# First attention pair of a fused kernel: products opened by the first matmul, zero-point term added by VectorE behind them

## The chip, the cores and the metric

The kernel runs on one core of a Trainium2 chip. Its engines are named as the profile names them: PE (TensorE, with PEld for its weight loads), DVE (VectorE), ACT (ScalarE), POOL (GpSimd) and SP (SyncE, which issues most DMAs). The metric is the device time of one execution in microseconds, as the median of several runs; less is better. Single instructions and stretches come from one execution that the hardware profiler recorded.

## What is computed

For each of two batches, an integer-quantised product of the layer-normalised x with a context matrix is added to x, and then a dense layer with LoRA terms is applied to the layer norm of that:

```python
def fake_quant(x, scale, zp):
    q = jnp.clip(jnp.round(x / s + z), 0.0, 255.0)
    return (q - z) * s
...
q1 = fake_quant(_layernorm(x), x1_scale, x1_zp)
q2 = fake_quant(ctx_4096, x2_scale, x2_zp)
x = x + jnp.matmul(q1, q2)
x = x + ffn(_layernorm(x), gate, kernel, bias, lora_A, lora_B, lora_A_shared, lora_B_shared)
```

x is (2, 1024, 2048), the context (2, 2048, 2048), all in float32. The change touches only the first part, and of it only the first of 32 products of its kind.

## The kernel before

**Tiles.** The 1024 tokens of a batch are eight tiles of 128, in four groups g of two tiles. The 2048 columns of the context are four blocks n of 512. A pair (b, n, g) is one call of `xattn_pair`: for each of the two token tiles j of group g, 16 matmuls over k = 0..15 (the 2048 inner rows in steps of 128) into one PSUM bank of 512 columns; the two banks are one tile `pa`.

**Operands.** The integers are centred at 128 so that both operands are exact in bf16. `prep_x` makes the left operand for one token tile: statistics on DVE (L283, L257), the short chain L259 to L290 on DVE with a square root on ACT (L261), quantisation on ACT (L295, to uint8 in the working tile `wk`; then L298 twice, to bf16 with row sums), 16 transposes on PE (L303) and two copies on DVE (L304) into `c1T[g]`; L307 and L308 make `r_s`, the tile's row sums times the context's offset. `quantise` makes the right operand, a slice r of two k steps at a time: ACT L314 from the loaded float slice in `lit` to int16 in `q2b`, DVE L317 from there to bf16 in `c2`. Eight slices make a block.

**Buffers.** `q2b` has three buffers, which `take` and `give` hand out in turn in the program's order. `quantise` takes one for each slice; `column_term` takes one between the slices of block 0 and those of block 1.

**Column term.** `column_term` (L327 to L348) sums the columns of a block: 16 narrow matmuls (`pcp`, L333), a copy on DVE into a q2b buffer (L343), one fp32 product with `mean_w` (`pc`, L345), and DVE L348, which scales it and adds a constant: `colt[n]`.

**The opening.** With zero points z1 and z2 a product is the centred product plus a term of the row and a term of the column. Before each group of 16 matmuls ACT writes this sum, `colt[n] + r_s[m]`, into the bank (L359), and the matmuls add to it, all with `start=False`. Behind the pair, DVE scales the two banks and adds them to x (L370), and takes statistics for the second norm (L372).

**Order.** For batch 0 the program calls, in this order: `prep_x` of tile 0, the eight slices of block 0 with `prep_x` of tile 1 after the fourth, the loads of x tiles 4 to 7, `column_term` of block 0, pair (0,0,0), slices 0 to 3 of block 1, `prep_x` of tiles 2 and 3, pair (0,0,1), the other slices and the column term of block 1, pairs (0,1,0) and (0,1,1); then tiles 4 to 7 with their pairs. `tc.issue_after(opened.ins)` sets the DVE instructions of tiles 4 to 7 behind the first pair's L370. The order on each engine's queue is not simply that of the program: a planner that works when the kernel is built sets it from the program's order, from what each instruction waits for and from its own costs, so that an instruction that it takes to be ready goes ahead of an earlier one that is not. In the trace, for instance, transposes of tile 3 stand among the first products of pair (0,0,1).

Of the kernel before, what the change touches and what calls it, by code (L numbers as in the profile page):

```python
# [14 lines left out]
AF = mybir.ActivationFunctionType  # L15
ALU = mybir.AluOpType
# [50 lines left out]
def tile_quant_xattn_then_lora_ffn(  # L67
# [17 lines left out]
    nc = tc.nc  # L85
# [11 lines left out]
    MG = GT // P  # L97
# [28 lines left out]
    r_s = const.tile([P, MT], F32, tag="r_s", name="r_s")  # L126
# [9 lines left out]
    def bf(t, n):  # L136

        return t.rearrange("p k n -> p (k n)").bitcast(BF16).rearrange("p (k n) -> p k n", n=n)
# [46 lines left out]
    def load_x(b, m, cols=slice(0, D)):  # L185
        nc.sync.dma_start(out=y[m // MG][:, m % MG, cols], in_=x[b, ds(m * P, P), cols])
# [90 lines left out]
    def prep_x(b, m, c1T, wk):  # L277

        nm = f"{b}_{m}"
        g, tok = m // MG, ds((m % MG) * P, P)  # L280
        ym = y[g][:, m % MG, :]
        for n in range(NN):
            nc.vector.bn_stats(st1[:, m, n, :], ym[:, ds(n * NB, NB)])  # L283
        mean, rstd = norm_stats(st1[:, m], f"a{nm}")

        k = small.tile([P, 1], F32, tag="kx", name=f"kx_{nm}")
        nc.vector.tensor_mul(k, rstd, inv1)
        o = small.tile([P, 1], F32, tag="ox", name=f"ox_{nm}")
        nc.vector.tensor_mul(o, mean, k)
        nc.vector.tensor_sub(o, z1, o)  # L290

        wf = flat(wk)
        q8 = wf[:, ds((m % 2) * (D // 4), D // 4)].bitcast(U8)
        qh = wf[:, D // 2 : D].bitcast(BF16)
        nc.scalar.activation(q8, ym, AF.Identity, bias=o, scale=k)  # L295
        rsum = small.tile([P, 2], F32, tag="rsum", name=f"rsum_{nm}")
        for h in range(2):
            nc.scalar.activation(  # L298
                qh[:, ds(h * H, H)], q8[:, ds(h * H, H)], AF.Identity, bias=n_centre, accum_out=rsum[:, h : h + 1]
            )  # L300
            pt = ps_m.tile([P, KH, P], BF16, tag="pm", name=f"pt_{nm}_{h}")
            for kt in range(KH):
                nc.tensor.transpose(pt[:, kt, :], qh[:, ds(h * H + kt * P, P)], ident_h)  # L303
            nc.vector.tensor_copy(c1T[g][:, ds(h * KH, KH), tok], pt)  # L304

        r_c = small.tile([P, 1], F32, tag="r_c", name=f"r_c_{nm}")
        nc.vector.tensor_add(r_c, rsum[:, 0:1], rsum[:, 1:2])  # L307
        nc.vector.tensor_mul(r_s[:, m : m + 1], r_c, d2)  # L308

    def quantise(c2, r):  # L310

        buf, t = next_loaded()
        qi = q2b.take()
        nc.scalar.activation(qi, t, AF.Relu, bias=z2, scale=inv2)  # L314
        lit.give(buf)
        load_next()
        nc.vector.tensor_scalar(c2[r // 4][:, ds(2 * (r % 4), 2), :], qi, QMAX, CENTRE, ALU.min, ALU.subtract)  # L317
        q2b.give(qi)
# [5 lines left out]
    colt = {}  # L324
    pairs = []

    def column_term(b, n, c2):  # L327


        parts = ps_m.tile([P, NB], F32, tag="pm", name=f"pcp_{b}_{n}")  # L330
        for k in range(KT):
            row = P // 4 * (k % 4)
            nc.tensor.matmul(  # L333
                parts[row : row + P // 4, :],
                ones_h[:, 0 : P // 4],
                c2[k // 8][:, k % 8, :],
                start=(k < 4),
                stop=(k >= KT - 4),
                skip_group_check=True,
            )  # L340
        st = q2b.take()
        sf = st.rearrange("p k n -> p (k n)").bitcast(F32)
        nc.vector.tensor_copy(sf, parts)  # L343
        pc = ps_m.tile([P, NB], F32, tag="pm", name=f"pc_{b}_{n}")
        nc.tensor.matmul(pc, mean_w, sf, start=True, stop=True)  # L345
        q2b.give(st)
        colt[n] = bp.take()
        nc.vector.tensor_scalar(colt[n], pc, d1, kdd, ALU.mult, ALU.add)  # L348

    def xattn_pair(b, n, g, c1T, c2):  # L350

        cols = ds(n * NB, NB)
        pairs.append((b, n, g))
        pa = ps_acc.tile([P, MG, NB], F32, tag=("acc0", "acc1", "delta")[len(pairs) % 3], name=f"pa_{b}_{n}_{g}")
        for j in range(MG):

            m = g * MG + j
            with tc.high_priority():
                nc.scalar.activation(pa[:, j, :], colt[n], AF.Identity, bias=r_s[:, m : m + 1])  # L359
            for k in range(KT):  # L360
                nc.tensor.matmul(  # L361
                    pa[:, j, :],
                    c1T[g][:, k, ds(j * P, P)],
                    c2[k // 8][:, k % 8, :],
                    start=False,
                    stop=(k == KT - 1),
                    skip_group_check=True,
                )
        yp = y[g][:, :, cols]
        summed = nc.vector.scalar_tensor_tensor(yp, pa, s12, yp, ALU.mult, ALU.add)  # L370
        for j in range(MG):
            nc.vector.bn_stats(st2[:, g * MG + j, n, :], y[g][:, j, cols])  # L372
        return summed
# [315 lines left out]
    c1T = [bf(t, GT) for t in c1T_bufs]  # L689
    wk = big.take()  # L690
    c2b = {}
    c2 = {}

    def open_c2(n):
        c2b[n], c2[n] = take_c2()
# [5 lines left out]
    for b in range(B):  # L701
# [6 lines left out]
        if b == 0:  # L708
            open_c2(0)
            prep_x(0, 0, c1T, wk)  # L710
            for r in range(NR):
                quantise(c2[0], r)
                if r == 3:
                    prep_x(0, 1, c1T, wk)
            for m in range(4, MT):
                load_x(0, m)
            open_c2(1)
            column_term(b, 0, c2[0])
        opened = xattn_pair(b, 0, 0, c1T, c2[0])
        if b == 0:  # L720
            for r in range(4):
                quantise(c2[1], r)
            for m in (2, 3):
                prep_x(b, m, c1T, wk)
        xattn_pair(b, 0, 1, c1T, c2[0])
        if b == 0:
            for r in range(4, NR):
                quantise(c2[1], r)
            column_term(b, 1, c2[1])
        for g in range(2):  # L730
            xattn_pair(b, 1, g, c1T, c2[1])
# [131 lines left out]
        if b + 1 < B:  # L863
            c1T_bufs, c1T, wk = state["c1b"], state["c1T"], state["wk"]
# [53 lines left out]
```

## Time and profile before

| | us |
|---|---|
| median of 3 runs (lowest to highest) | 1123.19 (1122.52 to 1124.55) |
| the profiled execution's own time | 1122.67 |
| its span, first instruction to last | 1120.9 |
| PE busy in the span | 1066.2 |
| DVE busy | 745.5 |
| ACT busy | 261.6 |
| pair (0,0,0): products on PE, first to last | 41.36 to 51.05 |
| mean of one L361 matmul, 128x512 bf16 (x992) | 0.381 |
| mean of one L359 opening, 128x512 (x64) | 0.683 |
| mean of one L370, 128x1024 (x32) | 1.282 |

The page gives for each engine its busy time and a row of 40 digits, each for 28 us of the span; other views list instructions in order of time, with the idle time before each and what ended it in square brackets, or sum up chosen stretches. A matmul's duration there contains its passage through the pipelined array, so that sixteen matmuls of 0.38 us take 3.61 us together. Some matmul records are missing, so a count can be short by a few per cent.

### The profile page before, as it was taken

The numbers are of one execution on the slowest core, as the hardware profiler recorded it, in microseconds if no ns is written. First come the engines' busy times: TensorE is split into PE (matmuls) and PEld (weight loads), VectorE is DVE, ScalarE is ACT, GpSimd is POOL, SyncE is SP. The second block draws the span as 40 slices with busy tenths as digits, with TensorE's granted clock in tenths as the row PEclk, the third lists the DMA queues.
The fourth block names the chain that finished last, engine by engine and source line by source line (L and its number), as shares of the span: only waits on it lengthen the run. The fifth ranks groups of instructions, "written<-read, shape, count | busy, mean of one in ns | idle before, by whom it ended". The sixth has DMA issues, their size and how long they took to land.

```text
span 1120.9 us, 10622 instructions
## 1 busy us (share of the span) xinstructions
PE 1066.2 (95%) x3898; PEld 493.9 (44%) x3930; DVE 745.5 (67%) x969; ACT 261.6 (23%) x358; POOL 260.7 (23%) x106
## 2 busy tenths in 40 slices
PE   1689999999999999999999999999999999999998
PEld 0344334554444444444444433455444444444443
DVE  4685547565697767668777654766568686865851
ACT  5875513220000000001375761232100000000000
POOL 0000000223353421534000000021534343253600
PEclk6799999999999999999999999999999999999999
DMA  8991946786789757499867095488768875749511
GB/s 307 393 248 36 281 127 233 265 319 234 246 283 374 281 175 261 153 328 322 286 187 226 1 280 151 180 301 313 253 225 293 302 260 175 260 145 322 208 38 56
DMA packets 120772, 261.35 MB, mean 233 GB/s; under 512 B 11920, under 2 KB 16144, under 8 KB 119568
## 3 DMA queue, kind: packets, MB, share of 16 engines
q1 hardware_dynamic: 99264, 218.65, 57.0%
q10 hardware_dynamic: 21456, 42.02, 11.0%
q8 instruction: 31, 0.51, 0.2%
q14 instruction: 21, 0.17, 0.0%
HBM read 224.99 MB, written 37.75 MB: 234 GB/s over the span
## 4 chain that ended last, share of the span: by engine, by line
PE 82%; DMA 7%; DVE 4%; ACT 4%; issue 1%; SPq 1%; ACTq 0%; DVEq 0%
PE fu L619 33%; PE fv L619 17%; PE pa L361 12%; PE fw L619 9%; DMA lit<-in_ctx_dram 4%; PE pl L491 3%; PE ptz L432 2%; DMA bd<-q2b 2%; DMA zs<-lit 1%; PE px L448 1%; PE pg_a L383 1%; DVE st L283 1%; PE pg_b L383 1%; ACT big L298 1%; ACT big L295 1%
## 5 line engine op out<-in xcount | busy, mean ns | idle before, releaser
L619 PE MATMUL fu<-big,lit 128*128 128x512 f32 x896 | 395.3, 593 | 0.0
L568 POOL TENSOR_TENSOR lit<-lit,lit 128x1024 f32<-128x1024 f32 x56 | 160.3, 2872 | 529.1 <-DMA zs<-lit 403.1
L619 PEld LDWEIGHTS fu<-big,lit 128*128 128x128 f32 x896 | 168.7, 190 | 206.2 <-issue 205.2
L361 PE MATMUL pa<-big,big 128*128 128x512 bf16 x992 | 233.3, 381 | 13.1 <-ACT pa L359 9.5
L619 PE MATMUL fv<-big,lit 128*128 128x512 f32 x448 | 198.1, 594 | 0.0
L559 POOL TENSOR_TENSOR lit<-lit,lit 128x1024 f32<-128x1024 f32 x40 | 99.8, 2497 | 293.6 <-DMA lit<-zs 261.9
L568 DVE TENSOR_TENSOR big<-big,big 128x2048 f32<-128x2048 f32 x56 | 161.5, 2888 | 5.7 <-PE ptz L432 5.1
L361 PEld LDWEIGHTS <-big 128*128 128x128 bf16 x1024 | 97.0, 98 | 144.5 <-issue 42.3
L637 DVE TENSOR_TENSOR y<-y,fu 128x1024 f32<-128x1024 f32 (+1 forms) x98 | 113.7, 1194 | 63.6 <-PE fu L619 63.3
L619 PEld LDWEIGHTS fv<-big,lit 128*128 128x128 f32 x448 | 84.3, 190 | 105.0 <-issue 104.7
L637 DVE TENSOR_TENSOR y<-y,fv 128x1024 f32<-128x1024 f32 x48 | 56.8, 1218 | 88.3 <-PE fv L619 88.3
L314 ACT ACTIVATE q2b<-lit,sc,inv 128x1024 int16<-128x1024 f32 x64 | 76.6, 1230 | 156.8 <-DMA lit<-in_ctx_dram 137.2
L559 DVE TENSOR_TENSOR big<-big,big 128x2048 f32<-128x2048 f32 x40 | 102.2, 2554 | 11.1 <-DMA big<-in_w_dram 11.1
L619 PE MATMUL fw<-big,lit 128*128 128x512 f32 x224 | 99.2, 592 | 0.0
L370 DVE SCALAR_TENSOR_TENSOR y<-pa,k_s,y 128x1024 f32<-128x1024 f32 x32 | 41.0, 1282 | 69.6 <-PE pa L361 69.6
L480 ACT COPY pl<-bias 128x1024 f32<-128x1024 f32 x16 | 16.3, 1018 | 293.9 <-DVE y L502 280.9
L359 ACT ACTIVATE pa<-bp,r_s 128x512 f32<-128x512 f32 x64 | 42.8, 683 | 105.4 <-PE pa L361 60.2
L619 PEld LDWEIGHTS fw<-big,lit 128*128 128x128 f32 x224 | 42.2, 190 | 51.8 <-issue 51.6
L637 DVE TENSOR_TENSOR y<-y,fw 128x1024 f32<-128x1024 f32 x24 | 28.4, 1217 | 50.5 <-PE fw L619 50.5
L303 PE MATMUL pt<-ident_h,big 128*128 128x128 bf16 x256 | 20.3, 231 | 29.7 <-ACT big L298 29.4
L283 DVE BATCH_NORM_STATS2 st<-y 128x6 f32<-128x512 f32 x64 | 42.0, 676 | 2.7 <-DMA y<-in_x_dram 2.7
L317 DVE TENSOR_SCALAR big<-q2b 128x1024 bf16<-128x1024 int16 x64 | 27.5, 439 | 22.6 <-ACT q2b L314 19.4
(82 smaller groups left out, 630.5 us busy)
## 6 DMA issues: line engine op xcount, KB each, us to landing
big<-in_w_dram SPq DMA_DIRECT2D x96, 1024.0 KB
lit<-zs SPq DMA_DIRECT2D x88, 512.0 KB
lit<-in_ctx_dram SPq DMA_DIRECT2D x64, 512.0 KB
out_dram<-y ACTq DMA_DIRECT2D x30, 512.0 KB
zs<-lit ACTq DMA_DIRECT2D x24, 512.0 KB
y<-in_x_dram SPq DMA_DIRECT2D x8, 1024.0 KB
lit<-in_lora_a_dram SPq DMA_DIRECT2D x32, 256.0 KB
lit<-in_lora_bt_dram SPq DMA_DIRECT2D x32, 256.0 KB
```

What stands on the lines that cost most here:

```text
L283: nc.vector.bn_stats(st1[:, m, n, :], ym[:, ds(n * NB, NB)])
L314: nc.scalar.activation(qi, t, AF.Relu, bias=z2, scale=inv2)
L317: nc.vector.tensor_scalar(c2[r // 4][:, ds(2 * (r % 4), 2), :], qi, QMAX, CENTRE, ALU.min, ALU.subtract)
L359: nc.scalar.activation(pa[:, j, :], colt[n], AF.Identity, bias=r_s[:, m : m + 1])
L361: nc.tensor.matmul(pa[:, j, :], c1T[g][:, k, ds(j * P, P)], c2[k // 8][:, k % 8, :], start=False, stop=(k == KT - 1), skip_group_check=True,)
L370: summed = nc.vector.scalar_tensor_tensor(yp, pa, s12, yp, ALU.mult, ALU.add)
L383: nc.tensor.matmul(ps[row : row + GP, :], gmat.rearrange("p i a r -> p (i a r)"), t[:, c, :], start=True, stop=True, skip_group_check=True,)
L491: nc.tensor.matmul(pl[j][i][:, half], axT[rows, pr, ds(j * P, P)], bt[rows, half], start=False, stop=True, skip_group_check=True,)
L559: line(eng.tensor_tensor(got[0], got[0], got[1], ALU.add if terms[1][2] > 0 else ALU.subtract))
L568: line(eng.tensor_tensor(out_t, at[p], at[q], op))
L619: nc.tensor.matmul(ps[:, m, :], at[:, k, ds(m * P, P)], bt[:, k, :], start=(opens and k == 0), stop=(ends and k == KQ - 1), skip_group_che ...
L637: line(nc.vector.tensor_tensor(yp, yp, chains[chain][:, js, :], ALU.add if sign > 0 else ALU.subtract))
```

## The change

For the first pair of batch 0 alone (`first_product`), the two openings by ACT are left out, and the first matmul of each group of 16 has `start=True`, which overwrites the bank. `column_term(b, 0, ...)` is no longer called ahead of the pair but inside it, behind its 32 matmuls in the program's order. Then, for each of the two banks, one DVE instruction adds `colt` and `r_s` to what the matmuls left: (colt + r_s) + pa, read from and written to PSUM. L370 and all other pairs are as before.

```diff
-    def xattn_pair(b, n, g, c1T, c2):
+    def xattn_pair(b, n, g, c1T, c2, first_product=False):
...
-            with tc.high_priority():
-                nc.scalar.activation(pa[:, j, :], colt[n], AF.Identity, bias=r_s[:, m : m + 1])
+            if not first_product:
+                with tc.high_priority():
+                    nc.scalar.activation(pa[:, j, :], colt[n], AF.Identity, bias=r_s[:, m : m + 1])
             for k in range(KT):
                 nc.tensor.matmul(
                     pa[:, j, :],
                     c1T[g][:, k, ds(j * P, P)],
                     c2[k // 8][:, k % 8, :],
-                    start=False,
+                    start=(first_product and k == 0),
                     stop=(k == KT - 1),
                     skip_group_check=True,
                 )
+        if first_product:
+            column_term(b, n, c2)
+            for j in range(MG):
+                m = g * MG + j
+                nc.vector.scalar_tensor_tensor(pa[:, j, :], colt[n], r_s[:, m : m + 1], pa[:, j, :], ALU.add, ALU.add)
...
             open_c2(1)
-            column_term(b, 0, c2[0])
-        opened = xattn_pair(b, 0, 0, c1T, c2[0])
+        opened = xattn_pair(b, 0, 0, c1T, c2[0], first_product=(b == 0))
```

## The prediction

> **What bounds the kernel now.** I read the page first: the shares of busy time, then the 40 slices.
>
> ```profile
> PE 1066.2 (95%) x3898; PEld 493.9 (44%) x3930; DVE 745.5 (67%) x969; ACT 261.6 (23%) x358; POOL 260.7 (23%) x106
> ...
> PE   1689999999999999999999999999999999999998
> ...
> PEclk6799999999999999999999999999999999999999
> ```
>
> PE is busy for 95% of the span, and what it is not busy lies almost wholly in the first three slices of 28 us. So anything that this change can win is a start: the moment from which PE runs without gaps must come sooner, and all behind it moves along. The next view is the busy time by stage (columns: stretch, its length, PE, weight loads, DVE, ACT, POOL, granted clock, DMA share, GB/s).
>
> ```profile
> 33.50:41.36 7.86, 5.02 (x35) 2.38 (x35) 7.24 (x18) 5.45 (x8) 0.00 (x0) 0.71 1.05 392
> 41.36:51.05 9.69, 8.69 (x34) 3.72 (x35) 3.66 (x21) 8.79 (x10) 0.00 (x0) 0.82 1.02 420
> 51.05:57.50 6.45, 5.31 (x48) 3.01 (x45) 6.41 (x13) 6.45 (x9) 0.00 (x0) 1.00 1.06 327
> 57.50:66.32 8.82, 5.76 (x34) 2.46 (x35) 8.80 (x19) 5.46 (x8) 0.00 (x0) 1.00 1.06 309
> 66.32:77.46 11.14, 10.25 (x46) 4.59 (x47) 8.31 (x31) 9.09 (x13) 0.00 (x0) 1.00 0.82 177
> 77.46:91.80 14.34, 13.93 (x88) 7.20 (x88) 7.39 (x25) 10.68 (x14) 0.00 (x0) 1.00 0.38 133
> ```
>
> From 66.32 on PE has hardly a gap (10.25 of 11.14, then 13.93 of 14.34). I take 66.32, where pair (0,1,0) begins, as the anchor: its shift is my forecast. Between 41 and 57 ACT is full (8.79 of 9.69, 6.45 of 6.45), between 51 and 66 DVE is (6.41 of 6.45, 8.80 of 8.82). The timeline then gives the chain around the first pair:
>
> ```profile
> 37.58 0.69 DVE L343 COPY q2b<-pcp 128x512 f32<-128x512 f32 x1
> ...
> 39.07 0.20 ACT L261 ACTIVATE sd_a<-ve_a 128x1 f32<-128x1 f32 x1 [2.20 <-DVE ve_a L259]
> ...
> 39.49 1.24 ACT L314 ACTIVATE q2b<-lit,sc,inv 128x1024 int16<-128x1024 f32 x1 [0.21 <-PE pc L345]
> 39.56 0.79 DVE L348 TENSOR_SCALAR bp<-pc,k_s 128x512 f32<-128x512 f32 x1
> ...
> 40.64 0.67 ACT L359 ACTIVATE pa<-bp,r_s 128x512 f32<-128x512 f32 x1
> ...
> 46.70 0.69 ACT L359 ACTIVATE pa<-bp,r_s 128x512 f32<-128x512 f32 x1 [0.45 <-PE pa L361]
> ```
>
> The reader is to see that the first product (41.36) waits for the whole column term, and that the second opening at 46.70 waits for the first 16 products to end. PE alone, further on:
>
> ```profile
> 47.44 3.61 PE L361 MATMUL pa<-big,big 128*128 128x512 bf16 x16 [0.78 <-ACT pa L359]
> ...
> 53.03 0.60 PE L361 MATMUL pa<-big,big 128*128 128x512 bf16 x2 [1.08 <-DVE big L304]
> ...
> 59.70 3.61 PE L361 MATMUL pa<-big,big 128*128 128x512 bf16 x15 [0.85 <-ACT pa L359]
> 63.15 1.02 PE L345 MATMUL pc<-q2b,mean_w 128*128 128x512 f32 x2
> 66.32 4.69 PE L361 MATMUL pa<-big,big 128*128 128x512 bf16 x21 [2.15 <-ACT pa L359]
> ```
>
> Pair (0,0,0) ends at 51.05, pair (0,0,1) runs from 53.03, its second half from 59.70, and each of these starts waits for ACT or for DVE copies of what ACT prepared.
>
> **First pair, begun earlier.** The ctx slices of block 0 are quantised by L317 at 15.95, 18.60, 22.38, 26.35, 27.01, 28.18, 29.27 and 32.38 us, and the transposed tile 0 is copied by 26.43 (25.74 + 0.69). PE is idle from 25.7 to 33.53. With no opening to wait for, 14 of the first 16 products fit there: the weight loads at half clock lie 0.43 apart (41.69, 42.11, 42.54), so 14 x 0.43 = 6.0, 25.7 to 31.7; the last two follow the eighth slice at 32.81. The second 16 need tile 1, whose copies end at 35.30 and 36.56: 16 x 0.226 (3.61 / 16) = 3.6, or 6.9 at half clock, so they end between 39 and 43, not at 51.05. I take 40.2: 35.4, 3.6, and 1.2 for the copy in the middle and a partly slow clock. PE's own lead is thus about 11 us, but the next work on PE is tile 2, which ACT has not prepared.
>
> **Column term, moved behind the products.** It is the same 16 pcp products, L343, pc and L348, and now they begin at 40.2: 1.05 (the 16 pcp at full clock, row at 115.17; 1.90 in the row at 35.63), 0.69, 1.12 and 0.3 between them give pc done at 43.3 rather than 39.45, and the column term at 44.1 after 0.80. Two things read what it leaves. One is pair (0,0,1)'s opening at 51.57, still 7 us later, so nothing. The other is the q2b buffer: three go round in program order, so the third slice of block 1 takes the one that pc reads, which is why L314 at 39.49 is released by pc. It is released some 3.9 us later now. Behind it on ACT stand L314 twice, a square root and L295 of tile 2 (44.17), and tile 2 is what PE needs next. If ACT's order is left as it was, the price is 3.9; if tile 2's L295 goes ahead of it, the price is 0, down to a small gain. I take 0.5, because the fill is there: L295 needs only ox of tile 2 from DVE, and DVE loses L343 (0.69) and L348 (0.79) from the stretch 37.5 to 40.4 in which that chain runs, so ox comes at about 42 rather than 43.55. I keep 0 and 3.9.
>
> **ACT, two openings less.** L359 at 40.64 and 46.70 go: 0.67 + 0.69, and with them the 0.45 of idle before the second: 1.8 us off the engine that is full from 41 to 57. This is the core of the gain.
>
> **DVE, two additions more.** SCALAR_TENSOR_TENSOR on 128x512 with PSUM as input and output isn't in the trace. L370 does 1024 in 1.28, so 0.64 is the lower bound; L348, 512 out of PSUM, takes 0.81; twice the lower one, 1.28, is the upper bound. I take 0.72 each, 1.4 in all, nearest to the row L502 (0.68 for 512 with one PSUM operand). They run at 44.1 to 45.6, where DVE was idle before (4.85 us before 49.71), so they cost nothing; without that cover 1.4. L370 of the first pair then ends at 46.9 instead of 52.37, which also takes it out of the way of tile 2's copy at 52.29 (0.3 to 1.0 gained for the start at 53.03, I take 0.7) and lets the statistics of tiles 4 to 7, which are ordered behind it, run in the gap rather than from 55.34 on. Their loads, four of 1 MB issued at 32.94 to 37 with the DMA at 1.0 of its share, must have landed by then: at about 0.4 MB/us four take 10 us, so 47 or a little later. If DVE stands for them, 0 to 2.
>
> **The clock.** PE has nothing to do between about 43.3 and tile 2's transposes near 46.5, and before only 1.1 of work in 38 to 41.4. The trace shows what follows (same columns):
>
> ```profile
> 40.00:41.00 1.00, 0.00 (x0) 0.00 (x0) 1.00 (x4) 1.00 (x2) 0.00 (x0) 1.00 1.06 414
> ...
> 42.00:43.00 1.00, 0.89 (x3) 0.34 (x3) 0.98 (x7) 0.55 (x2) 0.00 (x0) 0.50 1.10 459
> ...
> 45.00:46.00 1.00, 1.00 (x6) 0.47 (x5) 0.00 (x0) 1.00 (x1) 0.00 (x0) 1.00 0.98 410
> ```
>
> It went from 1.00 to 0.50 at 41.4, after that thin stretch, and back after 3.5 us of steady products. Today this lies in the first pair; the change moves it to pair (0,0,1). Seven or eight products at 0.43 instead of 0.226 are 1.4 to 1.6; transposes of tiles 2 and 3 at 1.05 instead of 0.6 per eight are up to 1.8 more. What covers it: PE waits 0.85 before 59.70 and ACT's next opening isn't due sooner. I charge 0.5 and keep 0 to 3.
> [...]
>
> **Sum.** -1.8 (openings) -0.7 (tile 2's copy) -1.0 (tile 2's ox earlier on ACT, less than the 1.5 worked out above since L314s are in front) +0.5 (q2b) +0.5 (clock) = -2.5 at 66.32. From there each PE start follows the last by the same work, so it reaches the end: profiled span 1120.9 - 2.5 = 1118.4, with the 1.8 around it (1122.67 - 1120.9) 1120.2 for that execution. The median 1123.19 stands 0.5 above it: 1120.7.
>
> **Rivals.**
> (a) *ACT held by q2b: slower.* One mechanism: the L314 of block 1's third slice stays in front of tile 2's L295, and ACT, which runs in order, stands until pc. For it: that is the order in the trace, and ACT sat idle there already (2.20 and 0.21). Against: nothing but that order keeps L295 behind. Price +3.9 to +7.5 (second 16 products and pcp at half clock: pc at 46.9), less 1.8: at 66.32 +2.1 to +5.7, so 1125.3 to 1128.9. It decides once pc is later than 41.3 (39.49 + 1.8) with that order kept. If the products are not put before tile 1's transposes at all, so that the change doesn't do what it says, pc comes later still and this is the likely end.
> (b) *The lead is carried further.* ACT's own work from 36.87 to block 1's last slice is 6 x 1.23 + 2 x 4.7 + 1.4 + 0.4 = 18.6, so 55.5 without idle; 0.43 + 0.15 + 0.69 + 1.12 + 0.80 + 0.67 and gaps of 0.5 put the anchor at 59.9, but PE needs about 10.5 from 50 on for pair (0,0,1), so 60.5 to 62: -4.3 to -5.8, 1117.4 to 1118.9. Against: pc at 63.15 stands behind the pair's second half today.
> (c) *Hidden.* The 1.8 is eaten by slow-clock products in pair (0,0,1) (up to 3) and by VectorE, at 10.0 of 10 from 60 to 70, which readies tile 4 for 77.46: -1 to +1, 1122.2 to 1124.2.
>
> **How the numbers follow.** Forecast, -1.2 to -4 (1119.2 to 1122.0): 0.50; (a) 0.25; (b) 0.15; (c) 0.10. A measurement of this kernel tells 0.2%, 2.2 us, from no change. Of the forecast's 0.50 some 0.35 lies below -2.2; with (b) faster is 0.50. The rest of it, 0.15, and (c) make same 0.25; slower 0.25. Eight in ten: down into (b), 1117.6, and up to 1125.6, into the nearer part of (a).
>
> **What would show it.** Right: first products from about 26 us, the first pair's products done by 43, L295 of tile 2 before 43.5, the start after tile 2 near 50.5, the clock low again around there, the anchor at 62.5 to 65. Wrong: an ACT idle of over 2 us ended by pc before tile 2's L295; DVE standing for x at the statistics of tiles 4 to 7; an anchor that moves without the end moving.

## The result, and the profile after

The changed kernel takes 1126.99 us as the median of 20 runs (1125.26 to 1130.89); the kernel before, on the same chips, 1123.16 (1121.25 to 1125.87, 20 runs). The ratio is 1.0036, with a 95% interval of 1.0029 to 1.0042: 3.8 us slower, not 2.5 faster. The profiled execution took 1128.59, with a span of 1126.8; it lies 1.6 above its own median, and the profiled one of before 0.5 below its own, so the two traces differ by 5.9 where the medians differ by 3.8.

From the page of the changed kernel, the rows that answer to those of before:

```profile
PE 1069.6 (95%) x3898; PEld 494.9 (44%) x3930; DVE 741.9 (66%) x971; ACT 260.3 (23%) x356; POOL 260.8 (23%) x106
...
PE   2489999899999999999999999999999999999998
```

The first slice of 28 us went from 1 to 2, the second from 6 to 4; of the rest only the eighth changed (9 to 8), far behind the change. So the first products did move forward, and the loss begins between 28 and 56 us. The busy time by stage (stretch, length, PE, weight loads, DVE, ACT, POOL, granted clock, DMA share, GB/s), over the same stretches as before:

```profile
33.50:41.36 7.86, 7.05 (x48) 3.24 (x48) 5.99 (x15) 4.95 (x8) 0.00 (x0) 0.78 1.06 396
41.36:51.05 9.69, 1.41 (x10) 0.30 (x2) 9.26 (x30) 6.74 (x6) 0.00 (x0) 0.71 1.01 414
51.05:57.50 6.45, 2.07 (x16) 1.54 (x16) 3.15 (x7) 6.45 (x8) 0.00 (x0) 0.50 1.06 328
57.50:66.32 8.82, 8.18 (x47) 3.89 (x49) 7.59 (x26) 4.51 (x10) 0.00 (x0) 0.71 1.04 307
66.32:77.46 11.14, 8.53 (x49) 4.09 (x49) 9.83 (x32) 9.93 (x12) 0.00 (x0) 1.00 0.43 125
```

In the second row PE fell from 8.69 to 1.41: that was the first pair, which is now done. What should have come forward into the hole did not. The row also shows who was busy instead: DVE went from 3.66 to 9.26, and ACT, which was the full engine there, stood for 3 of 9.69 us. The timeline of PE says where the hole ends:

```profile
25.74 4.09 PE L363 MATMUL pa<-big,big 128*128 128x512 bf16 x12
...
35.88 4.78 PE L363 MATMUL pa<-big,big 128*128 128x512 bf16 x15 [0.22 <-DVE st L283]
...
42.44 1.13 PE L345 MATMUL pc<-q2b,mean_w 128*128 128x512 f32 x2 [0.80 <-DVE q2b L343]
54.41 2.16 PE L303 MATMUL pt<-ident_h,big 128*128 128x128 bf16 x16 [10.84 <-ACT big L298]
...
74.56 10.52 PE L363 MATMUL pa<-big,big 128*128 128x512 bf16 x47 [0.40 <-ACT pa L361]
```

The first pair is done at 40.66 and its column term's product at 43.57, both as the prediction has them. Then PE waits 10.84 us for tile 2 (50.89 before, now 54.41), and pair (0,1,0) begins at 74.56 in place of 66.32. Of these 8.2 us 2.6 come back: the first `fu` product is at 197.4 instead of 191.8, 5.6 later. In part that is order and not gain, since tile 4's transposes now stand ahead of the pair (72.48 and 73.55) and before stood behind it (77.68). From the first `fu` product on the two traces run nearly alike, to 5.9 at the end.

Why tile 2 is late is to be read on DVE. Its timeline in the changed kernel (start, length, instruction, idle before it):

```profile
41.70 0.69 DVE L343 COPY q2b<-pcp 128x512 f32<-128x512 f32 x1 [1.43 <-PE pcp L333]
42.30 0.15 DVE L263 RECIPROCAL r_a<-sd_a 128x1 f32<-128x1 f32 x1
...
43.61 0.81 DVE L348 TENSOR_SCALAR bp<-pc,k_s 128x512 f32<-128x512 f32 x1
44.34 0.15 DVE L287 TENSOR_TENSOR kx<-rstd_a,inv 128x1 f32<-128x1 f32 x1
44.45 0.76 DVE L375 SCALAR_TENSOR_TENSOR pa<-bp,r_s,pa 128x512 f32<-128x512 f32 x1
...
45.45 0.75 DVE L375 SCALAR_TENSOR_TENSOR pa<-bp,r_s,pa 128x512 f32<-128x512 f32 x1
...
46.45 1.28 DVE L377 SCALAR_TENSOR_TENSOR y<-pa,k_s,y 128x1024 f32<-128x1024 f32 x1
47.64 0.15 DVE L289 TENSOR_TENSOR ox<-mv_a,kx 128x1 f32<-128x1 f32 x1
...
47.78 1.27 DVE L379 BATCH_NORM_STATS2 st<-y 128x6 f32<-128x512 f32 x2
48.96 0.14 DVE L290 TENSOR_TENSOR ox<-sc,ox 128x1 f32<-128x1 f32 x1
```

L263 to L290 is tile 2's chain: seven instructions of 0.10 to 0.20 us, each of which needs the last. In its gaps stands the tail of the first pair: L348, two additions (L375), the scale-and-add (now L377, L370 before) and the statistics (L379), 4.9 us in all. From L287 to L289, neighbours in the chain, 3.3 us pass. The first and the last of the chain in the kernel before, and the end of tile 3's:

```profile
40.60 0.15 DVE L263 RECIPROCAL r_a<-sd_a 128x1 f32<-128x1 f32 x1
...
43.40 0.16 DVE L290 TENSOR_TENSOR ox<-sc,ox 128x1 f32<-128x1 f32 x1
...
44.71 0.15 DVE L290 TENSOR_TENSOR ox<-sc,ox 128x1 f32<-128x1 f32 x1
49.71 0.16 DVE L307 TENSOR_TENSOR r_c<-rsum 128x1 f32<-128x1 f32 x1 [4.85 <-ACT big L298]
```

`ox` is complete at 49.10; before it was at 43.56. Of the 5.5 us between, 1.7 lie ahead of the chain: L263 starts at 42.30 and not at 40.60, because the copy L343 stands in front of it in DVE's queue and waits for PE (1.43). The other 3.8 are the tail, net of other DVE work that no longer stands there. ACT shows what hangs on that, first before, then in the changed kernel:

```profile
44.17 2.08 ACT L295 ACTIVATE big<-y,ox,kx 128x2048 uint8<-128x2048 f32 x1
```

```profile
43.61 1.24 ACT L314 ACTIVATE q2b<-lit,sc,inv 128x1024 int16<-128x1024 f32 x1 [2.90 <-PE pc L345]
...
46.57 2.37 ACT L314 ACTIVATE q2b<-lit,sc,inv 128x1024 int16<-128x1024 f32 x2 [0.49 <-DVE big L317]
49.14 4.08 ACT L295 ACTIVATE big<-y,ox,kx 128x2048 uint8<-128x2048 f32 x2 [0.20 <-DVE ox L290]
53.13 1.13 ACT L298 ACTIVATE big<-big,n_centre 128x1024 bf16<-128x1024 uint8 x1
```

There are three suspects in the four lines of the changed kernel: the 2.90 us for which ACT waits for `pc` (the q2b buffer, rival (a) of the prediction), L295 at 49.14 rather than 44.17 and ended by `ox`, and the two L295 of tiles 2 and 3 in one run (4.08), so that L298 of tile 2 stands behind tile 3. The experiments take them apart.

### The profile page after: what moved, and what is told of

Same layout as the page of the kernel before. It is cut to its first block, busy times and chain, and to the rows that moved or that the text cites. A ratio compares the mean times of both kernels' runs of the same rounds, so it can differ in the third digit from the quotient of the medians.

```text
span 1126.8 us, 10620 instructions
## 1 busy us (share of the span) xinstructions
PE 1069.6 (95%) x3898; PEld 494.9 (44%) x3930; DVE 741.9 (66%) x971; ACT 260.3 (23%) x356; POOL 260.8 (23%) x106
## 3 DMA queue, kind: packets, MB, share of 16 engines
q1 hardware_dynamic: 99264, 218.65, 55.9%
## 4 chain that ended last, share of the span: by engine, by line
PE 81%; DVE 4%; DMA 4%; ACT 3%; issue 1%; ACTq 0%; SPq 0%; DVEq 0%
PE fu L626 33%; PE fv L626 17%; PE pa L363 13%; PE fw L626 9%; PE pl L498 3%; PE ptz L439 2%; DMA bd<-q2b 2%; DMA zs<-lit 1%; PE px L455 1%; PE pg_a L390 1%; PE pg_b L390 1%; DVE st L283 1%; DMA lit<-in_ctx_dram 1%; DVE big L435 1%; ACT pa L361 1%
## 5 line engine op out<-in xcount | busy, mean ns | idle before, releaser
L575 DVE TENSOR_TENSOR big<-big,big 128x2048 f32<-128x2048 f32 x56 | 157.3, 2812 | 5.7 <-PE ptz L439 5.1
L566 DVE TENSOR_TENSOR big<-big,big 128x2048 f32<-128x2048 f32 x40 | 100.8, 2520 | 11.0 <-DMA big<-in_w_dram 11.0
L377 DVE SCALAR_TENSOR_TENSOR y<-pa,k_s,y 128x1024 f32<-128x1024 f32 x32 | 41.0, 1282 | 67.7 <-PE pa L363 67.7
```

Of the source, the lines that this page charges most:

```text
L566: line(eng.tensor_tensor(got[0], got[0], got[1], ALU.add if terms[1][2] > 0 else ALU.subtract))
L575: line(eng.tensor_tensor(out_t, at[p], at[q], op))
```

## The experiments

All ratios are to runs of the kernel before on the same chip, whose medians were 1123.31 (e1 to e4), 1123.95 (e5 to e8), 1123.44 (e9 to e12), 1123.85 (e13 to e16) and 1123.10 (e17, e18). A ratio is given with its 95% interval and need not be the quotient of the two medians. Instants are from one profiled execution of each kernel. Line numbers in quoted profiles are those of each experiment's own kernel, shifted by a few; `...` in code stands for lines left out.

**First set: the buffer, the place of the tail, the place of the column term, the additions.**

e1: the column term's copy goes into `axT`, a tile that isn't in use then, so no slice waits for `pc`.

```diff
-        st = q2b.take()
-        sf = st.rearrange("p k n -> p (k n)").bitcast(F32)
+        own = (b, n) == (0, 0)
+        st = axT if own else q2b.take()
+        sf = axT.rearrange("p a t -> p (a t)") if own else st.rearrange("p k n -> p (k n)").bitcast(F32)
...
```

> The changed kernel with one edit: the copy of the first column term's sums goes into a tile of its own (axT, unused until 200 us) instead of one of the three q2b buffers, so no L314 has to wait for pc. Theory V (VectorE's order: the first pair's column term, two additions, L377 and statistics stand ahead of tile 2's short chain, so its ox is ready at 49.1 instead of 43.6): ACT's wait of 2.90 us for pc goes, but ox of tile 2 stays at 48 to 49 and L295 with it; time 1126 to 1128, within 1 us of the changed kernel. Theory Q (the q2b wait on ACT is the cause): L295 of tile 2 moves forward by about 3 us and the time falls to 1122 to 1124.

Measured: 1127.46 us (8 runs), 1.0040 (1.0025 to 1.0056): no gain over the change. ACT in e1:

```profile
39.69 4.62 ACT L314 ACTIVATE q2b<-lit,sc,inv 128x1024 int16<-128x1024 f32 x4
...
48.72 4.08 ACT L295 ACTIVATE big<-y,ox,kx 128x2048 uint8<-128x2048 f32 x2 [0.48 <-DVE ox L290]
```

Four slices now run through without the wait for `pc`, and tile 2's L295 comes at 48.72 all the same, ended by `ox`. The wait was real, but taking it away won nothing: rival (a) had the right sign by the wrong mechanism. (Here `ox` still holds L295 up; e12 below tries the same with `ox` out of the way.)

e2: column term, additions, scale-and-add and statistics are called only after slices 0 to 3 of block 1 and `prep_x` of tile 2.

```diff
...
+                if m == 2:
+                    column_term(b, 0, c2[0])
+                    for j in range(MG):
+                        nc.vector.scalar_tensor_tensor(opened[:, j, :], colt[0], r_s[:, j : j + 1], opened[:, j, :], ALU.add, ALU.add)
+                    opened = finish_pair(0, 0, opened)
```

> The changed kernel, with the first pair's column term, its two additions, L377 and its statistics called only behind slices 0 to 3 of block 1 and prep_x of tile 2, so that VectorE does tile 2's chain first; q2b buffers in turn as before. Theory V: ox of tile 2 by 42 to 43, its transposes by 48, time 1117 to 1122, at or under the kernel before. Theory Q: pc still holds a q2b buffer, later still, and a later L314 stands for it; time 1125 or more. Theory C (clock: the loss is PE at half clock after a long idle): PE idles less, so about half of the loss comes back, 1124 to 1126.

Measured: 1125.08 (1.0015, 1.0005 to 1.0026). L295 starts at 42.85 and tile 2's transposes at 48.10. But the column term comes late too: pair (0,0,1) cannot open before 56.16, and pair (0,1,0) begins at 68.81. Somewhat more than half of the loss has gone.

e3: the column term is put ahead of the first products again, only additions and openings are as in the change.

```diff
+        if first_product:
+            column_term(b, n, c2)
         for j in range(MG):
...
-            column_term(b, n, c2)
```

> The changed kernel with the column term called ahead of the first pair's products again, as before; the products still begin slice by slice and the additions stay on VectorE. Theory Q: pc is over by about 40 and no L314 waits for it, time 1120 to 1123. Theory V: additions, L377 and statistics come right behind the products at 42 to 47 and ahead of tile 2's chain, ox not before 46; time 1124 to 1128.

Measured: 1127.54 (1.0033, 1.0021 to 1.0044). `pc` is done at 40.2 and L295 of tile 2 still comes at 50.11 only: the additions, scale-and-add and statistics run from 42.35 to 47.47, the chain's L263 only at 47.39, and `ox` is complete at 50.08. Where the column term stands is not the cause.

e4: the two additions are left out, and with them the zero-point term of the first pair.

```diff
-            for j in range(MG):
-                m = g * MG + j
-                nc.vector.scalar_tensor_tensor(pa[:, j, :], colt[n], r_s[:, m : m + 1], pa[:, j, :], ALU.add, ALU.add)
```

> The changed kernel without the two additions L375: the first pair's zero-point term is left out. Theory V with the additions as the main part: 1.5 us come back, 1125 to 1126; with the whole block (copy, L348, L377, statistics) as the cause: under 1.5 us, 1125.5 to 1127. Theory Q: no change, 1126.5 to 1127.5.

Measured: 1126.20 (1.0034, 1.0020 to 1.0048). `ox` comes at 47.12, 2.0 earlier than in the change and 3.6 later than before. So the added work is not the main part: without any of it the time is that of the change within the interval, which is too wide to exclude the 1.5 us of the two additions. What is left is old work that has become ready earlier: the scale-and-add now runs at 39.30 and the statistics at 41.07, both ahead of tile 2's chain, whose L263 comes at 44.76.

**Second set: the tail forced behind tile 2's chain.**

e5: the change with one order added: additions, scale-and-add and statistics of the first pair go behind tile 2's L290 on DVE. The column term stays where the change put it.

```diff
...
+                ready, last = prep_x(b, m, c1T, wk)
+                if m == 2:
+                    with tc.issue_after(ready.ins):
+                        for j in range(MG):
+                            nc.vector.scalar_tensor_tensor(opened[:, j, :], colt[0], r_s[:, j : j + 1], opened[:, j, :], ALU.add, ALU.add)
+                        opened = finish_pair(0, 0, opened)
```

> The changed kernel with one forced order: on VectorE the two additions, the first pair's L370 (scale and add to x) and its statistics come behind ox of tile 2 (L290); the column term stays behind the products as changed. Theory V: ox of tile 2 at about 44 instead of 49.1, its transposes at about 48 instead of 54.4; the loss of 3.8 us goes and part of the gain appears, 1120 to 1123.5. Theory Q (ACT's wait for pc): that wait is still there, so 1125 or more. A theory that the loss lies further back, in tiles 4 to 7: no change, 1126 to 1128.

Measured: 1122.81 (12 runs), 1.0004 (0.9985 to 1.0022): the loss is gone, within the interval, which does not meet that of the change. e9 and e12 to e16 below contain this edit, and none of them is clearly slower than the kernel before (0.9996 to 1.0014). DVE in e5, and then the L295 of tile 2 that it releases:

```profile
43.08 0.15 DVE L290 TENSOR_TENSOR ox<-sc,ox 128x1 f32<-128x1 f32 x1
43.15 0.75 DVE L738 SCALAR_TENSOR_TENSOR pa<-bp,r_s,pa 128x512 f32<-128x512 f32 x1
...
44.92 1.28 DVE L381 SCALAR_TENSOR_TENSOR y<-pa,k_s,y 128x1024 f32<-128x1024 f32 x1
```

```profile
43.27 2.09 ACT L295 ACTIVATE big<-y,ox,kx 128x2048 uint8<-128x2048 f32 x1 [0.27 <-DVE ox L290]
```

The same instructions in the other order: `ox` at 43.23, and then the tail. Part of the 5.9 us between this and 49.10 is the execution: `pc` ended 1.8 earlier in it (the last section says why). Counted from `pc`, `ox` comes 1.5 us later here and 5.5 in the change, and the medians, of 12 and 20 runs, don't hang on one execution. Tile 2's transposes begin at 47.77, 6.6 sooner than in the change. This settles the loss. But the kernel is only level with the one before, not faster, and PE in e5 shows that the head start is gone by 66 us:

```profile
47.77 2.16 PE L303 MATMUL pt<-ident_h,big 128*128 128x128 bf16 x16 [6.05 <-ACT big L298]
51.58 0.58 PE L364 MATMUL pa<-big,big 128*128 128x512 bf16 x1 [1.65 <-ACT pa L362]
...
60.04 3.63 PE L364 MATMUL pa<-big,big 128*128 128x512 bf16 x15
63.50 1.02 PE L346 MATMUL pc<-q2b,mean_w 128*128 128x512 f32 x2
66.48 4.48 PE L364 MATMUL pa<-big,big 128*128 128x512 bf16 x20 [1.96 <-ACT pa L362]
```

Pair (0,0,1) starts at 51.58, 1.45 earlier than before, its second half at 60.04 (59.70 before), and pair (0,1,0) at 66.48 (66.32 before). Half the question is left: what ate it.

e6 is e5 with the column term ahead of the products (as e3); e8 is e6 with the tail behind tile 3's L290 (`if m == 3`); e7 is the change, with only tile 3's ACT instructions forced behind tile 2's last L298:

```diff
...
+                if m == 3:
+                    with tc.issue_after(prepped.ins):
+                        prep_x(b, m, c1T, wk)
...
```

> As the last one (additions and the first pair's L370 behind ox of tile 2 on VectorE), and the column term called ahead of the products again as before the change. Theory V: VectorE doesn't stand for pcp before tile 2's chain and ACT doesn't stand for pc: ox of tile 2 by 43, transposes at 46.5, 1118 to 1122, under the kernel before. If what the moved column term costs is nothing, the same as the last one within 1 us.

> The changed kernel with another forced order, on ACT alone: the instructions of prep_x of tile 3 come behind tile 2's second L298, since in the changed kernel both L295 stand ahead of the first L298 (in the kernel before L298 of tile 2 came first). Theory V with the order on ACT as its second half: tile 2's L298 begins 2.08 us sooner, at 51 or before, 1124.5 to 1126.5. If ox alone makes the loss: no change, 1126 to 1128.

> As the second of these (column term first), but the additions and L370 of the first pair behind ox of tile 3. Theory V: tile 3's L295 can follow tile 2's L298 without a wait, at or below the second one, 1117 to 1122. If VectorE's order past tile 2 doesn't matter, the same within 1 us.

Measured: e6 1124.92 (1.0008, 0.9998 to 1.0018), e8 1126.31 (1.0020, 1.0007 to 1.0032), e7 1127.45 (1.0035, 1.0022 to 1.0049). In e7 the L295 no longer stand in one run (2.09, then L298 at 51.53), yet the time is the change's: putting the third suspect right wins nothing, though tile 3 pays for it (its transposes come at 63.62 instead of 57.80). In e6 and e8 the tail is out of tile 2's way as well, and nothing is won over e5. e8 is even slower than the kernel before: its tail, held back until 48.54, now stands ahead of tile 2's copies (51.52), and pair (0,0,1) begins at 54.34 only.

**Third and fourth set: what eats the head start.** The candidates were the half clock that PE has in tile 2's transposes and in pair (0,0,1) (0.50 from 45.7 to 55.9 in e5), the order of tile 2's preparation, the q2b buffer (with the tail out of the way), the statistics of tiles 4 to 7, and the column term's copy. e9 puts 22 matmuls of no use between `pc` and tile 2's transposes of e5, to hold the clock; e13 another 10 behind these transposes:

```diff
...
+                    with tc.issue_after(pcs[0, 0].ins):
+                        for _ in range(22):
+                            nc.tensor.matmul(warm[:, 0, :], ones_h, ones_h[:, 0:1].to_broadcast([P, NB]), start=True, stop=True)
```

e10 calls `prep_x` of tile 2 ahead of the first pair, with the tail behind its L290, and e11 adds e7's order to that. e12 is e5 with e1's buffer. e14 is e5 with DVE's work for tiles 4 to 7 behind the second pair's L370 (`opened = second`), e15 is e5 with the copy L343 behind tile 2's L290, e16 both of these.

> The kernel with the additions behind ox of tile 2 (1122.8, level with the kernel before), and 22 idle matmuls of ones on PE between pc and tile 2's transposes, into a bank that nothing uses until later, to keep the clock up. Theory C (there the lead of 1.45 us at pair (0,0,1) is lost to the half clock: transposes at 2.16 instead of 1.06 per 16, and products at 0.43, so that the pair's first half ends at 58.2 instead of 57.5): the clock stays at 1.00, the first half of the pair ends at 56 to 57, and 1 to 2 us come off, 1120.5 to 1122. If ACT or block 1's slices set the second half anyway: second half still at about 59 to 60, no change, 1122 to 1124.

> The changed kernel with prep_x of tile 2 called ahead of the first pair in the program's order, and additions and the first pair's L370 behind ox of tile 2. Theory V: what bounds the start is tile 2's preparation on VectorE and ACT, so ox comes at 41 or before, tile 2's transposes by 46, 1117 to 1122. If the column term's delay is what counts (colt for the next opening), it ends at or above the kernel before, 1123 to 1126.

> As the last one, with tile 3's instructions on ACT behind tile 2's second L298, which without this stands behind both L295. Theory V: tile 2's transposes 2 us sooner than in the last one, but tile 3's later by as much; with PE idle in front of tile 2, 0.5 to 1.5 us better than it. If tile 3 or block 1's slices set pair (0,1,0): no better, or worse by up to 2.

> The kernel with the additions behind ox of tile 2, and the column term's copy in a tile of its own instead of a q2b buffer. Theory Q, in its remaining part (1.38 us on ACT before an L314 at 41.76): up to 1.4 us come off, 1121 to 1122. Theory V: L295 waits for ox, not for that L314, so within 1 us of 1122.8.

> The kernel with the additions behind ox of tile 2, with 22 idle matmuls of ones on PE between pc and tile 2's transposes and 10 more between these and pair (0,0,1). Theory C: the clock is 1.00 from 39 on, the pair's first half takes 4.5 us instead of 6.6 and ends by 57, the second half begins by 58.5, 1 to 2 us come off: 1120.5 to 1122. Theory S (block 1's last slice sets the second half): its products still begin at about 60, no change, 1122 to 1124.

> The kernel with the additions behind ox of tile 2, and VectorE's part of prep_x of tiles 4 to 7 behind the second pair's L370 instead of the first's. Theory S: block 1's last slice and column term come sooner, pair (0,1,0) begins by 65, but tile 4 may come later than 77; 1120 to 1123. Theory C: no change at (0,1,0), 1122 to 1125.

> The kernel with the additions behind ox of tile 2, and the copy of the first column sums (L343), and with it everything that follows of the column term, behind ox of tile 2 too. If the stand for pcp and the copy hold up tile 2: ox at 41.5 to 42 instead of 43.3, tile 2's transposes at 46, 1 to 1.5 us come off, 1120.5 to 1122. If it is hidden: 1122 to 1124.

> Both of the last two. If the parts add up: 1119.5 to 1121.5, under the kernel before by 2 to 4. If the start is bound by ACT's own work and tile 4: 1122 to 1124.

| | median us | ratio (95%) | pair (0,1,0) begins |
|---|---|---|---|
| e9, 22 idle matmuls | 1124.48 | 1.0011 (0.9994 to 1.0027) | 68.30 |
| e10, tile 2 prepared first | 1123.29 | 1.0001 (0.9990 to 1.0012) | 68.22 |
| e11, and tile 3 behind it | 1126.22 | 1.0027 (1.0016 to 1.0037) | 68.38 |
| e12, own buffer | 1125.25 | 1.0014 (0.9999 to 1.0029) | 68.42 |
| e13, 32 idle matmuls | 1123.25 | 0.9996 (0.9982 to 1.0010) | 66.59 |
| e14, statistics late | 1123.11 | 0.9998 (0.9989 to 1.0007) | 66.84 |
| e15, copy late | 1123.98 | 1.0008 (0.9995 to 1.0021) | 66.98 |
| e16, both late | 1124.79 | 1.0008 (0.9992 to 1.0023) | 66.94 |

None is faster than the kernel before, and e11 is slower. The start of pair (0,1,0) does not go with the time: e10 begins it 1.9 us later than the kernel before and is level. e9 is inconclusive, since its clock fell to 0.50 at 52 in spite of the idle matmuls (the last section), and e13 is half so: the transposes took 0.62 us for eight, as at full clock, but the ten matmuls behind them took 4.01 us, 0.40 each against 0.23 for the 22 ahead of the transposes (4.95 us), and pushed the pair's first half to 54.30, where it then took 4.5 us rather than the 6.6 of e5. The row to look at is e16, where pair (0,0,1) came earliest. PE in e16:

```profile
50.77 0.59 PE L365 MATMUL pa<-big,big 128*128 128x512 bf16 x1 [1.55 <-ACT pa L363]
...
58.58 3.63 PE L365 MATMUL pa<-big,big 128*128 128x512 bf16 x15
62.14 0.40 PE L335 MATMUL pcp<-big,ones_h 128*32 128x512 bf16 x3
64.18 1.13 PE L347 MATMUL pc<-q2b,mean_w 128*128 128x512 f32 x2 [1.65 <-DVE q2b L345]
66.94 8.29 PE L365 MATMUL pa<-big,big 128*128 128x512 bf16 x24 [1.63 <-ACT pa L363]
```

The pair's second half begins at 58.58, 1.1 us before that of the kernel before, and pair (0,1,0) is 0.6 later. Between them lies block 1's column term: its last three narrow products, the copy, `pc`, L348, the opening. That chain is what the anchor waits for in each of e9 to e16: it begins 2.8 to 3.3 us behind the start of `pc`, released by its opening. In e15 and e16, where the pair's second half did come sooner, the gain is used up by the wait for the copy ahead of `pc` (1.65 in e16).

**Fifth set: the anchor's own wait.** e17 is e5 in which pair (0,1,0), too, begins without openings, with two additions behind its products, so that no product of it waits for a column term. e18 is the kernel before with this alone; the first pair is opened by ACT as it was.

```diff
...
-            xattn_pair(b, 1, g, c1T, c2[1])
+            xattn_pair(b, 1, g, c1T, c2[1], first_product=(b == 0 and g == 0))
```

> Kernel of e5 in which block 1's first pair (0,1,0), the anchor, also begins without an opening: its products start from zero, and its zero-point column is added by VectorE behind them, so that no product of it waits for block 1's column term (last slice, copy of pcp, pc, L349, opening; 66.48 in e5, of which 63.67 to 66.48 held 1.0 us of PE work). Theory C (that column term's chain behind the second half of pair (0,0,1) is what holds the anchor and so ate the head start): the wait of 1.96 us before the pair goes, products of it that need only block 1's first slices go into PE's idle time before 60 us, and the time falls by 2.0 to 6 us against the kernel before: 1117.5 to 1121.5. Theory D (PE's end is set by ACT and VectorE preparing tiles 2 to 5 whatever PE does): PE's gaps only move, pair (0,1,1) or tile 4 is waited for instead; 1121.5 to 1124.5. Two more additions on VectorE, 0.75 us each, are in both.

> The kernel before, first pair opened as it was, with only pair (0,1,0) begun without an opening and its zero-point column added behind its products. Theory C: the same gain without the change under study, 1117 to 1121.5, since the wait at 66.32 (2.15 us before it) goes and products of the pair fill earlier gaps of PE. Theory D: level, 1121.5 to 1124.5. If e17 is faster than e18 by 1 us or more, the early first products are worth something once the anchor's own wait is gone; if they are equal, they are worth nothing here.

Measured, against 1123.10 of the kernel before: e17 1117.12 (5 runs, 1115.85 to 1117.71), 0.9944 (0.9931 to 0.9956); e18 1117.96 (5 runs, 1115.71 to 1118.81), 0.9953 (0.9940 to 0.9967). Both are some 5 to 6 us faster than the kernel before, and 9 to 10 faster than the changed one. PE in e18:

```profile
37.21 0.95 PE L362 MATMUL pa<-big,big 128*128 128x512 bf16 x2
...
57.96 4.54 PE L362 MATMUL pa<-big,big 128*128 128x512 bf16 x20
62.34 1.02 PE L345 MATMUL pc<-q2b,mean_w 128*128 128x512 f32 x2
63.19 7.50 PE L362 MATMUL pa<-big,big 128*128 128x512 bf16 x34
```

At 37.21 two products of pair (0,1,0) stand in the gap ahead of the first pair: block 1's first slices and tile 0 are there, and nothing else was needed. Behind `pc` PE goes on at once (63.19), where it stood for 2.15 us before. The gain is larger than that wait. Up to `pc` the trace has 78 products, at least 14 more than the 64 of the first two pairs, so by an estimate some 3 us of the pair (14 x 0.226) fill earlier gaps; and in this execution the clock stays at 1.00 in 41.36 to 51.05, where it was 0.82 before. How the 5 us divide among these, and the two openings that ACT saves, was not separated. Busy time by stage, first e18, then e17, over the stretch in which the kernel before had 5.76 of 8.82 and e5 6.44:

```profile
57.50:66.32 8.82, 8.82 (x45) 3.90 (x39) 8.82 (x21) 4.80 (x7) 0.00 (x0) 1.00 1.05 316
```

```profile
57.50:66.32 8.82, 8.82 (x52) 3.83 (x50) 8.20 (x22) 4.12 (x6) 0.00 (x0) 0.99 1.04 312
```

PE is full there in both. Of the two theories, the column term as the anchor's bound stands, and "set by ACT and VectorE preparing tiles 2 to 5 whatever PE does" falls. The medians of e17 and e18 differ by 0.84 with intervals that overlap; whether the first pair's head start is worth anything once this wait is gone was not told apart.

## Why the prediction was wrong

It said 1120.7, faster, range 1117.6 to 1125.6. The time was 1126.99.

- *First pair, begun earlier*: right. Products from 25.74 (about 26), the pair done at 40.66 (40.2), `pc` at 43.57 (43.3).
- *Two additions on DVE*: right in size, 0.76 and 0.75 each (0.72), with L377 ending at 47.73 (46.9). **This is the step that failed, in its place: "They run at 44.1 to 45.6, where DVE was idle before (4.85 us before 49.71), so they cost nothing".** The trace of before has DVE idle only from 44.86 on, when the chains of tiles 2 and 3 were finished, so the first half of that stretch was not idle even there. In the changed kernel the tail becomes ready at 43.6, in the middle of tile 2's chain, and it stands earlier in the program's order than that chain; what the planner then laid down had it in the chain's gaps. The same holds for L370, which was booked as a gain for ending early. The runs showed in its place an `ox` 5.5 us later (49.10 for 43.56), 3.8 of them by the tail, and a time 3.8 us longer: e5 moves only the additions, L377 and the statistics behind the chain, and the loss is gone; e4, without the additions, keeps most of it.
- *`ox` at about 42*: 49.10, by the same failure. It was worked out from what DVE loses from the stretch (L343, L348), not from what it gains there. With the tail out of the way (e5) it came at 43.23 and L295 at 43.27, 0.9 sooner than before: the -1.0 that the sum takes for this was there then, and the kernel was level all the same.
- *Column term and q2b*: the wait came about as rival (a) has it (2.90 us on ACT, ended by `pc`), but e1 and e12 take it away without a gain. The rival's range, 1125.3 to 1128.9, holds the result by another cause, which is luck; and the sign named for it, ACT idle for over 2 us until `pc`, was seen though it was not the cause. Of the two idle times cited for it in the trace of before, 2.20 and 0.21, only the 0.21 was ended by `pc`; the 2.20 was ended by DVE's `ve_a`.
- *ACT, two openings less, 1.8 off*, called the core of the gain: they went, and e5, where nothing is given back on DVE, is still level. **The second failed step is "Sum"**: it subtracts from the start at 66.32 what ACT and DVE save further forward, as if everything between moved with them. 66.32 was released by the opening behind block 1's column term, behind the second half of pair (0,0,1); e5 and e13 to e16 begin there 0.2 to 0.7 us later than before, though pair (0,0,1) begins 1.45 sooner in e5 and 2.3 in e16. The objection is in the prediction, under rival (b) ("pc at 63.15 stands behind the pair's second half today"), and was used against the rival but not against the forecast. e17 and e18 confirm it. Nor does the anchor's shift reach the end whole, as the sum has it: of the changed kernel's 8.2 us 5.6 are left at the first `fu` product, and e10, with an anchor 1.9 later, is level.
- *The clock*: right that it is low again further on: 0.50 from 45.5 to 62.6 in the changed kernel. There it lies mostly on the transposes of tiles 2 and 3 (2.16 and 2.17 us for 16, against 1.06 for tile 2's before) and only on the first products of pair (0,0,1). In e5 it lies on that pair, whose first half took 6.6 us at partly half clock against 4.5 before; since e5 is level with the kernel before, these 2.1 us were not what made the loss. The price of the half clock could not be isolated (e9, e13).

What stays open: what the half clock costs, and with it whether the first pair's head start is worth anything. e18 holds the clock at 1.00 through 44 to 56, with the first pair opened as before; e17 has the head start but 0.50 from 47.4 to 57.7, and the two are level. No run had the head start and the clock together without other work in the way.

## What to carry to other kernels

Work that becomes ready sooner is not free on an engine that takes its queue in order (in the changed kernel DVE's L263, whose input was there at 39.58, started at 42.30, behind a copy that waited 1.43 us for PE), even if the trace of before shows the engine idle: ask whose short dependent chain is running when it gets ready, and if a planner orders by readiness and program order, force the bulky tail behind that chain. Before summing savings to an anchor, name the one event that releases the anchor and check that each saving lies on the way to it; here one operand of the anchor, the column term, could be taken off its path by adding it afterwards, and that was worth 5 to 6 us where the same trick on the first pair, once its tail was out of the way, was worth nothing that could be measured.

## What the runs showed of the hardware

In three executions the granted clock fell to 0.50 behind 3.0 us in which PE was thinly busy, not wholly idle. The busy time by stage in e9 (columns as above):

```profile
49.00:50.00 1.00, 0.62 (x8) 0.45 (x8) 0.90 (x6) 1.00 (x3) 0.00 (x0) 1.00 0.94 387
50.00:51.00 1.00, 0.62 (x8) 0.53 (x9) 0.93 (x5) 0.98 (x3) 0.00 (x0) 1.00 1.01 399
51.00:52.00 1.00, 0.00 (x0) 0.02 (x1) 1.00 (x3) 1.00 (x1) 0.00 (x0) 1.00 1.02 385
52.00:53.00 1.00, 0.00 (x0) 0.00 (x0) 1.00 (x3) 1.00 (x3) 0.00 (x0) 0.50 1.05 387
```

The 3.0 us before the fall at 52 held 1.24 us of transposes, and the longest gap in them was about 1 us. In the kernel before, the 3.0 us before the fall at 41.4 held 1.09 us of matmuls (longest gap 1.9 us), and in the changed kernel those before the fall at 45.5 held 1.07 (1.9 us). So in these three the fall came behind a thin stretch; how thin or how long it has to be was not shown.

The transposes followed the granted clock: eight took 0.62 us at 1.00 (the rows above) and 1.06 at 0.50 (49.54 to 50.60 in e17). Whether they hold the clock up was not tested: e9's clock fell after a stretch with transposes alone, and the two others after as little work in other matmuls. One reading goes against this: e5's profile has a mean granted clock of 0.95 over the first 110 us, which the 0.50 from 45.7 to 55.9 alone accounts for, so about 1.00 is left for the rest; yet 16 transposes at 23.45 took 2.16 us there, and the 14 products behind them 4.84 rather than 3.2 (14 x 0.226). In the changed kernel 12 of these products took 4.09 us, with the clock at 0.50 from 24 to 28.

The same 16 products of the first pair's second half took 3.40 us in e5 and 4.78 in the changed kernel, with a mean granted clock over 33.50 to 41.36 of 1.00 and 0.78, and 4.87 in e9. Runs of e5 spread from 1121.1 to 1130.87, those of e17 from 1115.85 to 1117.71.
